# Masked attention with a residual: other slots for the indirect gathers, the copies that hold them and the searches ahead of them

## The chip, the cores and the metric

The kernel runs on one core of a Trainium2 chip. The metric is the device time in microseconds (us), lower is better. In the profiles PE is the matrix engine (PEld its weight loads), DVE the vector engine, ACT the scalar engine, POOL the general engine, and SP the engine whose queue issues most of the plain transfers. POOL issues the indirect transfers, in which a list of row numbers in SBUF says which rows of a DRAM tensor are read.

## The reference

`x` has 8 batches of 512 features by 1024 tokens, `cond_2048` is a mask of 8 by 1024 zeros and ones, and Wq and Wo are 512 by 512. There are 8 heads of 64 features.

```
xt = transpose(x, (0, 2, 1))
q = xt @ Wq.T                                   # queries, keys and values are the same
scores = einsum('bhqd,bhkd->bhqk', qh, qh) / sqrt(64)
logits = (scores * cmask + (1 - cmask) * -1e30) * rmask
attn = softmax(logits)
ctx = einsum('bhqk,bhkd->bhqd', attn, qh)
out = x + transpose(ctx @ Wo.T, (0, 2, 1))
```

A masked key has no weight in a kept row; a masked query has logits of zero everywhere, so that its context is the mean of all values. About half of the tokens are kept.

## The kernel before

Only kept tokens are attended. For every batch the kernel finds the kept tokens, gathers their rows of `x` and computes attention for up to 536 of them (a second version for 576 is in the program and isn't executed here). One further column stands for the mean token, which serves all masked queries. Rows of the result are added to `x` by another set of indirect transfers, which read for each of the 1024 tokens the row of its own kept place or the mean's row.

A **pair** is a batch and two of its eight heads: `(b, pr)` with pr 0 to 3, so there are 32. A pair has five **slots** c = 0 to 4. In slot c PE multiplies the scores of 128 keys (24 in the last) with all queries (`scores`, L684, the last one L698), ACT makes exponentials of them (`e`, `el`, L707), and PE weighs the values of the slots before (`weigh`, L731). Between these a pair's slots also prepare the next pair: in slots 0 and 1 its queries are projected (`pq`, L550) and copied to `qT` by ACT and DVE (L567); behind slot 2 PE turns `qT` into values (`turn_values`, L588) and DVE copies them to `v` (L597, two copies); then come their squares on ACT, the largest length on DVE (`len`, `top`), a small matmul (L628) and the bias `m`, `bias` (L637 to L641), which the next pair's first exponential needs.

Between the pairs' own work the function `plan` puts tasks into slots: `put(batch, pair, slot, task, ..., rank)`. Inside one slot tasks run in the order of their rank, with ranks under 5 ahead of the rest. The order of each engine's instructions is what `late` writes while it walks through pairs and slots; nothing is reordered later. An engine that waits holds everything behind it in its own row. The tasks that matter here are these:

- `search(n, i)` (DVE, L464 and L467): for piece i of batch n, i = 0 to 4, one pass over the token ranks counts and finds the source rows. The pass is over 1024, 896, 768, 640 and 512 columns for i = 0 to 4.
- `gather(n, i)` (POOL, L478): an indirect transfer `xin<-xd` of the rows that `search(n, i)` found. It stands for n = 2 to 7 in batch n-1. `collect(n, i)` turns the gathered piece on PE (L491) in the fourth slots of pairs 1 and 2 of the same batch.
- `wait_for_values(pair)` (POOL, L471): POOL copies two elements of row 0 of the pair's values `v` to a scratch tile `tick`. The copy can't run until DVE has written both halves of `v`, so POOL's later instructions are held until then.
- `fetch(b, i)` (POOL, L1084): an indirect transfer that adds rows of the output `od` of batch b to `g`, which `load_rows` has filled with rows of `x` two slots or more before. There are 8 per batch, for b = 0 to 4 in batch b+2. Later `finish_blocks(b, i)` (DVE, L1054) transposes `g` into `whole`, from which the result is stored.
- In every pair POOL also issues four small transfers `row<-rt` (L822), which carry the inverse sums of the pair before through DRAM. They wait for DVE's `rt` (L819).
- `half_product` (PE, L930, sixteen or eight matmuls of 256 columns) stands in the fourth slots; its sums are made by DVE (`joined`, L954) and written to `od` by POOL (L971).

Of the kernel before, what the change touches and what calls it, by code (L numbers as in the profile page):

```python
# [305 lines left out]
def attention_of_kept_tokens(ctx, tc, x, mask, wq, wo, out, ident, wqT, woT, verdict, flag):  # L306
# [7 lines left out]
    ND = D // P  # L314
# [6 lines left out]
    NC = -(-LONG // P)  # L321
    LAST = NC - 1
# [43 lines left out]
    xs, xbars, xmeans, xins, xcs, searches = {}, {}, {}, {}, {}, {}  # L366
# [106 lines left out]
    def gather(b, i):  # L473
        n = sizes[i]
        if i == 0:
            xins[b] = []
        xin = sb.tile([P, D], F32, tag="xin", name=f"xin_{b}_{i}", bufs=NC)
        nc.gpsimd.indirect_dma_start(  # L478
            out=xin[:n, :],
            out_offset=None,  # L480
            in_=rows_of_x[b],
            in_offset=bass.IndirectOffsetOnAxis(ap=searches[b][2][:n, i : i + 1], axis=0),
        )
        xins[b].append(xin)

    def collect(b, i, tag="t", copy=None):
        n = sizes[i]
# [842 lines left out]
    def plan():  # L1330
# [5 lines left out]
        def put(b, pr, c, task, *args, rank=0):  # L1336
            todo[b, pr, c].append((rank, task, args))
# [17 lines left out]
        for n in range(1, B):  # L1355
            if n == 1:
                turns = [(0, 0, 0), (0, 0, 1), (0, 0, 3), (0, 0, 4)]
                finds = [(0, 1, 0), (0, 1, 3), (0, 1, 3), (0, 1, 4), (0, 2, 0)]
                feats = [None] * (ND + 2) + [(0, 0, 4), (0, 1, 0)]
                takes = finds  # L1360
                means, mean = (0, 2, 1), (0, 2, 3)
                turned = [(0, 2, 3)] * NC
            else:
                b = n - 2
                if n == 2:
                    loads = [(0, 1, i) for i in range(NC)] + [(0, 2, i) for i in range(3)]
                    turns = [(0, 2, 3), (0, 2, 4), (0, 3, 1), (0, 3, 3)]
                    feats = [(0, 2, 3)] * 2 + [(0, 2, 4)] * 2
                    feats += [(0, 3, 0), (0, 3, 1), (0, 3, 2), (0, 3, 4)]
                else:  # L1370
                    loads = [(b, 0, i) for i in range(4)]
                    loads += [(b, 1, 0), (b, 1, 2), (b, 1, 4), (b, 2, 0)]
                    turns = [(b, 1, 1), (b, 2, 1), (b, 2, 3), (b, 3, 1)]
                    feats = [(b, 1, 1), (b, 1, 4), (b, 2, 1), (b, 2, 4), (b, 2, 4)]
                    feats += [(b, 3, 1), (b, 3, 4), (b, 3, 4)]
                for i in range(NN * A):
                    put(*loads[i], load_piece, n, i // A, i % A)
                put(b, 2, 0, load_ranks, n)
                finds = [(b + 1, 0, min(i, 3)) for i in range(NC)]
                takes = [(b + 1, 0, 0)] + [(b + 1, 0, 3)] * (NC - 1)  # L1380
                put(b + 1, 0, 3, wait_for_values, (b + 1, 1), rank=1)
                means, mean = (b + 1, 0, 1), (b + 1, 0, 3)
                turned = [(b + 1, 1, 3)] * 2 + [(b + 1, 2, 3)] * 2 + [(b + 1, 1, 3)]
            for i in range(NQ):
                put(*turns[i], turn, n, i, rank=6.8 if turns[i][2] == LAST - 1 else 1)
            for i in range(NN * ND):
                if feats[i]:
                    put(*feats[i], add_features, n, i, rank=1)
            for i in range(NC):
                put(*finds[i], search, n, i)  # L1390
                put(*takes[i], gather, n, i, rank=2)
                if i in (0, 2):
                    put(*turned[i], collect, n, i, rank=7)
                else:
                    put(*turned[i], collect, n, i, "t", nc.scalar.copy, rank=7.2)
            put(*means, mean_of, n)
            put(*mean, put_mean, n, rank=6.5)

        for b in range(B - 1):
            nxt = b + 1  # L1400
            steps = ((1, 2), (6, 5), (7, 4, LAST + P), (3,))
            at = [(nxt, 1), (nxt, 2), (nxt, 3), (nxt + 1, 0)]
            if b == B - 3:
                steps = ((1, 2), (6, 5, LAST + P), (7, 3, 4))
            elif b == B - 2:
                steps = ((1, 2, 6, 5, 4, 7, 3, LAST + P),)
            for i, step in enumerate(steps):
                for k in step:
                    task, k = (output, k - P) if k > P else (half_product, k)
                    put(*at[i], 3, task, b, k, rank=7.1)  # L1410
                    if b == B - 2 and task is half_product and k == 5:
                        for j in (2, 3):
                            put(*at[i], 3, mix_contexts, b, j, rank=7.1)
            if b < B - 2:
                put(nxt, 1, 3, mix_contexts, b, 0, rank=6.8)
                put(nxt, 1, 3, mix_contexts, b, 1, rank=6.8)
                put(nxt, 3, 2, mix_contexts, b, 2, rank=5.5)
                put(nxt, 3, 2, mix_contexts, b, 3, rank=5.5)
            else:
                for k in range(2):  # L1420
                    put(nxt, 1, 1 + k, mix_contexts, b, k, rank=5.5)
            if b < B - 3:
                after = [(nxt + 1, i // NC, i % NC) for i in range(4 * NC)]
                firsts, slots = after[3:], after[6:]
                ends = [(2, 0), (2, 3), (2, 3), (2, 4), (3, 0), (3, 3), (3, 3), (3, 3)]
                ends = [(nxt + 1, *at) for at in ends]
            elif b == B - 3:
                firsts = [(nxt, 2 + i // NC, i % NC) for i in range(2, 2 + NT)]
                slots = [(nxt + 1, 0, i // 2) for i in range(NT)]
                ends = [(1, 0), (1, 0)] + [(1, 3)] * (NT - 2)  # L1430
                ends = [(nxt + 1, *at) for at in ends]
            else:
                firsts = [(nxt, 1 + i // NC, i % NC) for i in range(NT)]
                slots = [(2, 1), (2, 1), (2, 2), (2, 3), (2, 4), (3, 0), (3, 0), (3, 1)]
                slots = [(nxt, *at) for at in slots]
                ends = [(nxt, 3, c) for c in (0, 0, 3, 3, 3, 3, 3, 3)]
            for i in range(NT):
                put(*firsts[i], load_rows, b, i, rank=1)
                put(*slots[i], fetch, b, i, rank=3)
            for i, at in enumerate(ends):  # L1440
                put(*at, finish_blocks, b, i, rank=(2, 2, 2, 6.8, 4.5)[at[2]])
# [16 lines left out]
    def late(n):  # L1458
# [7 lines left out]
        for i in range(NC):  # L1466
            gather(0, i)
# [25 lines left out]
        blank_share(pairs[0])  # L1493

        todo = plan()
        settled = defaultdict(list)
        for p in range(len(pairs) - 2):
# [154 lines left out]
```

## Time and profile before

| what | value |
|---|---|
| median of three runs | 663.98 us (663.39 to 664.54) |
| profiled execution | 657.5 us |
| its span | 655.7 us |
| mean granted clock of PE | 0.975 |
| PE busy | 595.9 us (91%) |
| DVE busy | 404.6 us (62%) |
| ACT busy | 349.0 us (53%) |
| POOL busy | 241.9 us (37%) |

The span is the time between the first and last instruction of the profiled execution. "Idle before, releaser" in a row of groups says how long the engine was idle just before these instructions and what ended most of that time. In a row of the timeline the first two numbers are start and duration in us, and the bracket holds the idle time just before. A row of windows gives a stretch, its length and each engine's busy time with its count of instructions, then PE's granted clock, the busy share of the transfer engines and GB/s. The stretches that are used run from the first exponential of a pair to that of the next.

### The profile page before, as it was taken

How to read it: one execution, taken by the hardware profiler on the slowest of the kernel's cores; microseconds unless marked ns; L12 is line 12 of the kernel's file. 1: busy time of each engine (PE TensorE's matmuls, PEld its weight loads, DVE VectorE, ACT ScalarE, POOL GpSimd, SP SyncE). 2: the span in 40 equal slices, each digit the busy share in tenths (PEclk: the TensorE clock that was granted, in tenths of full speed). 3: DMA queues.
4: the chain of work that ended last, by engine and by line, in shares of the span. 5: the costliest groups of instructions: out<-in, count | busy, mean ns of one | idle time of the engine just before them, and what ended most of it. 6: DMA issues, size and time to landing. Idle time of an engine off the chain costs nothing.

```text
span 655.7 us, 22452 instructions
## 1 busy us (share of the span) xinstructions
PE 595.9 (91%) x9296; PEld 446.3 (68%) x9296; DVE 404.6 (62%) x1191; ACT 349.0 (53%) x986; POOL 241.9 (37%) x327
## 2 busy tenths in 40 slices
PE   6689898999999999999989998999989999998862
PEld 4556765778777776788757785678757776785431
DVE  6546678556766677577755776467745564765242
ACT  5266686566555565556656564556545446436300
POOL 4501433211344334541453324551353525537040
PEclk9799999999999999999999998999999999999985
DMA  8746545422389758975887678774756648798555
GB/s 278 241 130 185 188 112 173 132 95 73 101 238 230 161 161 253 245 194 113 239 255 217 120 211 270 181 184 103 183 192 134 139 129 213 150 289 135 148 167 168
DMA packets 100161, 116.89 MB, mean 178 GB/s; under 512 B 13224, under 2 KB 67048, under 8 KB 100040
## 3 DMA queue, kind: packets, MB, share of 16 engines
q1 hardware_dynamic: 76176, 76.56, 39.6%
q0 software_dynamic: 19520, 36.58, 23.8%
q10 hardware_dynamic: 4344, 2.12, 1.1%
q8 instruction: 77, 1.26, 0.8%
q14 instruction: 44, 0.36, 0.2%
HBM read 72.68 MB, written 42.54 MB: 176 GB/s over the span
## 4 chain that ended last, share of the span: by engine, by line
PE 74%; DVE 7%; DMA 5%; issue 4%; POOL 3%; ACT 3%; SPq 1%; another core or an unknown queue 1%; DVEq 0%; POOLq 0%; ACTq 0%
PE av L731 17%; PE s L684 16%; PE pq L550 15%; PE ph L930 12%; DMA g<-od,origin 3%; PE v L588 3%; PE xc L491 3%; POOL g L1084 3%; PE s L698 2%; PE pa L987 2%; DVE junk L464 1%; DVE joined L954 1%; ACT e L707 1%; DMA out_dram<-whole 1%; DMA x<-in_x_dram 1%
## 5 line engine op out<-in xcount | busy, mean ns | idle before, releaser
L707 ACT ACTIVATE e<-s,bias 128x536 f32<-128x536 f32 x256 | 178.2, 700 | 64.0 <-PE s L684 55.9
L731 PE MATMUL av<-e,v 64*64 64x268 f32 x2048 | 168.3, 392 | 18.5 <-ACT el L707 4.8
L684 PE MATMUL s<-qT 64*64 64x268 f32 x2048 | 171.1, 390 | 4.1 <-ACT el L707 2.2
L822 POOL DMA_DIRECT2D row<-rt x120 | 63.1, 549 | 233.3 <-DVE rt L819 229.5
L550 PE MATMUL pq<-xc,wqT 64*64 64x268 f32 (+1 forms) x1984 | 136.0, 386 | 0.6 <-DVE m L637 0.4
L731 PEld LDWEIGHTS av<-e,v 64*64 64x64 f32 x2048 | 88.1, 133 | 55.6 <-ACT el L707 7.2
L684 PEld LDWEIGHTS s<-qT 64*64 64x64 f32 x2048 | 100.4, 133 | 30.1 <-ACT el L707 6.2
L550 PEld LDWEIGHTS pq<-xc,wqT 64*64 64x64 f32 x1984 | 97.3, 133 | 21.8 <-DVE m L637 2.2
L1084 POOL DMA_INDIRECT g<-od,origin x48 | 76.3, 1589 | 18.1 <-issue 14.3
L597 DVE COPY v<-v 128x320 f32<-128x320 f32 x64 | 28.4, 485 | 54.9 <-PE v L588 38.9
L707 ACT ACTIVATION_READ_ACCUMULATOR e<-s,bias 128x1 f32 x256 | 50.1, 196 | 0.0
L478 POOL DMA_INDIRECT xin<-xd,source x40 | 38.6, 965 | 26.8 <-issue 7.3
L707 ACT ACTIVATE el<-s,bias 128x268 f32<-128x268 f32 x64 | 30.3, 479 | 31.8 <-PE s L698 13.0
L464 DVE TENSOR_SCALAR_CACHE_REDUCE junk<-rank,key 128x1024 f32<-128x1024 f32 (+4 forms) x40 | 39.8, 996 | 2.8 <-DMA rank<-ranks 2.8
L954 DVE TENSOR_TENSOR joined<-ph,side 128x512 f32<-128x512 f32 x28 | 19.2, 690 | 35.0 <-PE ph L930 23.7
L427 ACT ACTIVATE junka<-x 128x512 f32<-128x512 f32 x64 | 40.2, 628 | 0.7
L930 PE MATMUL ph<-wo,mix 128*128 128x256 f32 x168 | 39.8, 385 | 0.2 <-DVE joined L954 0.2
L1054 DVE STREAM_TRANSPOSE whole<-g 128x512 f32<-128x512 f32 x56 | 36.4, 683 | 2.3 <-DMA g<-od,origin 2.2
L765 ACT COPY cT<-av 128x268 f32<-128x268 f32 x62 | 22.3, 383 | 28.4 <-PE av L731 28.3
L930 PEld LDWEIGHTS ph<-wo,mix 128*128 128x128 f32 x168 | 30.5, 190 | 7.5 <-issue 1.6
L971 POOL DMA_DIRECT2D od<-joined x14 | 10.9, 776 | 64.3 <-DVE joined L954 64.3
L401 DVE STREAM_TRANSPOSE xt<-x 128x1024 f32<-128x1024 f32 x28 | 34.2, 1224 | 0.2
(179 smaller groups left out, 813.4 us busy)
## 6 DMA issues: line engine op xcount, KB each, us to landing
xd<-xt SPq DMA_DIRECT2D x120, 128.0 KB
x<-in_x_dram SPq DMA_DIRECT2D x56, 256.0 KB
g<-xd SPq DMA_DIRECT2D x48, 256.0 KB
out_dram<-whole SPq DMA_DIRECT2D x20, 512.0 KB
rb<-row SPq DMA_DIRECT2D x60, 160.0 KB
od<-joined POOLq DMA_DIRECT2D x14, 512.0 KB
out_dram<-whole SPq DMA_DIRECT2D x16, 256.0 KB
rank<-ranks SPq DMA_DIRECT2D x7, 512.0 KB
```

Source lines behind the costliest of these rows:

```text
L401: nc.vector.transpose(xt.rearrange("p k (d f) -> p k d f", d=ND), xs[b][r][:, :, at : at + n].rearrange("p d (k t) -> p k d t", t=Q),)
L427: nc.scalar.activation(junk, xs[b][r][:, d, :], AF.Copy, accum_out=xbars[b][:, d, r : r + 1])
L464: nc.vector.tensor_scalar(junk[:, :n], rank[:, i * P :], key[:, col], 0.0, ALU.is_le, ALU.add, accum_out=found[:, col])
L478: nc.gpsimd.indirect_dma_start(out=xin[:n, :], out_offset=None, in_=rows_of_x[b], in_offset=bass.IndirectOffsetOnAxis(ap=searches[b][2][:n ...
L550: mm = nc.tensor.matmul(pqs[pair][hf][heads[h], :n], wqT[rows, d, at : at + DK], xcs[b][rows, d, hf * KH : hf * KH + n], start=(not cross ...
L684: nc.tensor.matmul(s[h][to, hf, :KH], qT[heads[h], at : at + DK], qT[heads[h], hf * KH : (hf + 1) * KH], start=True, stop=True,)
L707: act = nc.scalar.activation(e[:, h], of[h], AF.Exp, bias=biases[pair][:, c : c + 1], scale=SCALE, accum_out=acc[:, h, c : c + 1],)
L731: mm = nc.tensor.matmul(avs[pair][hf][heads[h], :KH], v[rows, c, heads[h]], e[rows, h, hf, :] if c < LAST else e[rows, h, :], start=(c == ...
L822: nc.gpsimd.dma_start(row[:, :, a, :].rearrange("h c j -> (h c) j"), rt[a * Q : a * Q + 2 * NC, :])
L930: nc.tensor.matmul(po[:, t * m : (t + 1) * m], left[:, i, t * P : (t + 1) * P], right[:, i, :], start=(i == 0), stop=(i == 1),)
L1054: nc.vector.transpose(whole.rearrange("p (d a) n -> p a d n", a=A)[:, :, :, i * Q : (i + 1) * Q], gs.pop((b, i)).rearrange("p (a d f) -> p ...
L1084: nc.gpsimd.indirect_dma_start(out=gs[b, i], out_offset=None, in_=ods[b], in_offset=bass.IndirectOffsetOnAxis(ap=origin[:, b, i : i + 1] i ...
```

## The change

Five things are changed in `plan` and one in `gather`.

- The five searches of batch n (n of 2 and more) stood in slots 0, 1, 2, 3, 3 of pair 0 of batch n-1. Now searches 0 and 1 stay, search 4 stands in slot 2, search 2 in slot 3, and search 3 in slot 4 at rank 4.6, behind the bias and share of the next pair.
- The five gathers stood in slot 0 (the first) and slot 3 (the other four) of pair 0. Now gather 0 stands in slot 0, gather 1 in slot 1, gathers 2 and 4 in slot 3, and gather 3 in slot 0 of pair 1.
- `wait_for_values` stood in slot 3 of pair 0 alone. Now it stands in slot 3 of pairs 0, 1 and 2.
- The eight fetches of b = 0 to 4 stood one to a slot in slots 1 to 4 of pair 1 and 0 to 3 of pair 2. Now three stand in slot 3 of pair 1, one in slot 0 of pair 2, three in slot 3 of pair 2 and one in slot 0 of pair 3. Their transposes and loads stay.
- `xins[b]` becomes a dictionary, since gathers no longer come in the order of i.

```diff
     def gather(b, i):
         n = sizes[i]
         if i == 0:
-            xins[b] = []
+            xins[b] = {}
...
-        xins[b].append(xin)
+        xins[b][i] = xin
...
-                finds = [(b + 1, 0, min(i, 3)) for i in range(NC)]
-                takes = [(b + 1, 0, 0)] + [(b + 1, 0, 3)] * (NC - 1)
-                put(b + 1, 0, 3, wait_for_values, (b + 1, 1), rank=1)
+                finds = [(b + 1, 0, c) for c in (0, 1, 3, 4, 2)]
+                takes = [(b + 1, 0, 0), (b + 1, 0, 1), (b + 1, 0, 3), (b + 1, 1, 0), (b + 1, 0, 3)]
+                for pr in range(ND - 1):
+                    put(b + 1, pr, 3, wait_for_values, (b + 1, pr + 1), rank=1)
...
             for i in range(NC):
-                put(*finds[i], search, n, i)
+                put(*finds[i], search, n, i, rank=4.6 if n > 1 and finds[i][2] == LAST else 0)
                 put(*takes[i], gather, n, i, rank=2)
...
             if b < B - 3:
                 after = [(nxt + 1, i // NC, i % NC) for i in range(4 * NC)]
-                firsts, slots = after[3:], after[6:]
+                firsts = after[3:]
+                slots = [(1, 3)] * 3 + [(2, 0)] + [(2, 3)] * 3 + [(3, 0)]
+                slots = [(nxt + 1, *at) for at in slots]
```

PE's, ACT's and SP's rows keep their order. The first place is POOL's row in pair 0 of a batch, from the `row` transfers of the pair before to the output's `joined`; `xin_0` to `xin_4` are the five gathers of the next batch, `tick_1` the copied element of pair 1's values. Before:

```order
L822 DMA row_3_3702<-rt_3_3700 10x32 x4
L478 DMA xin_0_3712<-xd_97,source_3171 128x512
L471 COPY tick_1_3848<-v_1_3789 1x2
L478 DMA xin_1_3852<-xd_97,source_3171 128x512
L478 DMA xin_2_3854<-xd_97,source_3171 128x512
L478 DMA xin_3_3856<-xd_97,source_3171 128x512
L478 DMA xin_4_3858<-xd_97,source_3171 24x512
L971 DMA od_3581<-joined_0_3049 128x2x512
```

Now the same stretch reads:

```order
L822 DMA row_3_3710<-rt_3_3708 10x32 x4
L478 DMA xin_0_3720<-xd_97,source_3176 128x512
L478 DMA xin_1_3750<-xd_97,source_3176 128x512
L471 COPY tick_1_3855<-v_1_3799 1x2
L478 DMA xin_2_3859<-xd_97,source_3176 128x512
L478 DMA xin_4_3861<-xd_97,source_3176 24x512
L971 DMA od_3589<-joined_0_3055 128x2x512
```

One gather has moved ahead of the copied element, two are left behind it, and `xin_3` is gone from the stretch. The second place is POOL's row in pairs 1 to 3 of the same batch, where `g_0` to `g_7` are the eight fetches and `row_0` to `row_2` the row transfers. Before:

```order
L822 DMA row_0_3968<-rt_0_3966 10x32 x4
L1084 DMA g_0_3850<-od_3581,origin 128x512
L1084 DMA g_1_3894<-od_3581,origin 128x512
L1084 DMA g_2_3975<-od_3581,origin 128x512
L1084 DMA g_3_4001<-od_3581,origin 128x512
L822 DMA row_1_4241<-rt_1_4239 10x32 x4
L1084 DMA g_4_4051<-od_3581,origin 128x512
L1084 DMA g_5_4105<-od_3581,origin 128x512
L1084 DMA g_6_4167<-od_3581,origin 128x512
L1084 DMA g_7_4251<-od_3581,origin 128x512
L822 DMA row_2_4510<-rt_2_4508 10x32 x4
L971 DMA od_4656<-joined_1_4647 128x2x512
```

Now:

```order
L822 DMA row_0_3974<-rt_0_3972 10x32 x4
L478 DMA xin_3_3983<-xd_97,source_3176 128x512
L471 COPY tick_2_4111<-v_2_4060 1x2
L1084 DMA g_0_3857<-od_3589,origin 128x512
L1084 DMA g_1_3897<-od_3589,origin 128x512
L1084 DMA g_2_3981<-od_3589,origin 128x512
L822 DMA row_1_4250<-rt_1_4248 10x32 x4
L1084 DMA g_3_4009<-od_3589,origin 128x512
L471 COPY tick_3_4385<-v_3_4334 1x2
L1084 DMA g_4_4058<-od_3589,origin 128x512
L1084 DMA g_5_4113<-od_3589,origin 128x512
L1084 DMA g_6_4177<-od_3589,origin 128x512
```

Each of pairs 1 and 2 now has one transfer directly behind its `row` transfers and three behind a copied element. The third place is what follows on POOL, and there the eighth fetch has moved into pair 3, behind the third set of row transfers:

```order
L822 DMA row_2_4521<-rt_2_4519 10x32 x4
L1084 DMA g_7_4260<-od_3589,origin 128x512
L971 DMA od_4668<-joined_1_4659 128x2x512
L886 DMA od_4668<-oc_4_4670 24x128 x4
L822 DMA row_3_4789<-rt_3_4787 10x32 x4
```

On DVE only the searches move, by up to a slot and a half within pair 0, as the first of the points above says.

## The prediction

> **What bounds the kernel.** I read the page's chain first, then its groups, to see who waits for PE where PE is the chain:
>
> ```profile
> PE 74%; DVE 7%; DMA 5%; issue 4%; POOL 3%; ACT 3%; SPq 1%; another core or an unknown queue 1%; DVEq 0%; POOLq 0%; ACTq 0%
> ...
> L1084 POOL DMA_INDIRECT g<-od,origin x48 | 76.3, 1589 | 18.1 <-issue 14.3
> L597 DVE COPY v<-v 128x320 f32<-128x320 f32 x64 | 28.4, 485 | 54.9 <-PE v L588 38.9
> ```
>
> PE carries three quarters of the chain, and DVE's value copies stand idle 38.9 us for its value matmuls. What the change moves, POOL's gathers (1589 ns each in L1084's row), is hardly on the chain, so they mostly act through what PE, DVE and ACT do while POOL makes descriptors. The timeline shows such an action. Here is pair 2 of batch 2 and then the same place in batch 3:
>
> ```profile
> 215.32 0.23 PE L588 MATMUL v<-ident,qT 64*64 64x64 f32 x2
> 213.47 1.66 POOL L1084 DMA_INDIRECT g<-od,block_origin  x1 [0.30 <-DMA g<-xd]
> 215.43 1.58 POOL L1084 DMA_INDIRECT g<-od,block_origin  x1 [0.30 <-DMA xd<-xt]
> 216.86 0.89 DVE L597 COPY v<-v 128x320 f32<-128x320 f32 x2 [3.15 <-PE s L684]
> 287.72 0.23 PE L588 MATMUL v<-ident,qT 64*64 64x64 f32 x2
> 288.06 0.89 DVE L597 COPY v<-v 128x320 f32<-128x320 f32 x2 [1.95 <-PE v L588]
> 288.33 1.65 POOL L1084 DMA_INDIRECT g<-od,origin  x1 [2.77 <-DMA xd<-xt]
> ```
>
> In batch 2 the last value matmul ends at 215.55, and an idle DVE starts its copy only at 216.86, 1.31 us later and at the end of the gather that began at 215.43. In batch 3 POOL was held up until 288.33 by chance; the copy came 0.11 us behind the matmul (287.95 to 288.06). So PE's completion reaches others late while a gather is being issued. The stretches of the pairs (pair 2 of batches 2, 3, 5 and 6, then pair 3 of batch 2, which has no gather) give the price:
>
> ```profile
> 207.07:226.24 19.17, 18.48 (x293) 14.34 (x289) 12.50 (x33) 11.38 (x33) 8.46 (x8) 1.00 0.92 222
> 279.47:297.43 17.96, 17.96 (x292) 14.60 (x288) 12.49 (x33) 11.25 (x33) 8.45 (x8) 1.00 0.76 191
> 427.65:446.82 19.17, 18.46 (x294) 13.99 (x289) 12.50 (x33) 11.37 (x34) 8.45 (x8) 1.00 0.75 179
> 502.08:522.03 19.95, 19.03 (x318) 14.80 (x314) 10.43 (x31) 9.71 (x29) 10.60 (x12) 1.00 0.53 114
> 226.24:244.00 17.76, 17.76 (x312) 14.33 (x308) 13.62 (x36) 10.88 (x34) 4.93 (x9) 1.00 0.42 117
> ```
>
> Batches 3 and 5 do the same work with the same transfer share (0.76, 0.75). Where all four fetches came behind the copy, the pair took 17.96 us and PE never stood idle; where the first two preceded it, 19.17. That is 1.2 us for the place alone. Fetches in the fourth slot cost nothing there.
>
> **What each pair loses now.** Pair 0, batches 1 to 6:
>
> ```profile
> 101.47:118.31 16.84, 13.99 (x276) 9.46 (x272) 12.19 (x43) 8.75 (x26) 7.06 (x10) 1.00 0.57 173
> 172.10:188.94 16.84, 16.06 (x282) 11.66 (x277) 12.77 (x44) 8.84 (x27) 7.83 (x11) 1.00 0.49 135
> 244.00:261.02 17.02, 16.19 (x281) 11.79 (x276) 12.77 (x44) 8.83 (x26) 7.86 (x11) 1.00 0.82 251
> 315.20:332.86 17.66, 15.68 (x272) 11.11 (x267) 13.19 (x48) 8.94 (x27) 7.84 (x11) 1.00 0.84 264
> 388.94:408.50 19.56, 16.34 (x276) 11.87 (x272) 12.85 (x45) 8.95 (x26) 7.84 (x11) 0.91 0.87 273
> 464.57:483.02 18.45, 16.04 (x270) 11.19 (x266) 13.19 (x47) 8.94 (x26) 7.84 (x11) 1.00 0.75 240
> ```
>
> Their floor I build from pair 3, whose 17.76 us hold two half-products and a small output; pair 0 has one half-product (none in batch 1). The chain prices these:
>
> ```profile
> 236.25 3.65 PE ph L930 x16
> 239.90 1.01 PE po L874 x32
> 254.36 1.92 PE ph L930 x8
> ```
>
> 17.76 - 3.65 - 1.01 + 1.92 = 15.0; with an allowance of 0.3 (estimate) for the mean's products the floor is 15.3, and 13.4 in batch 1. Pair 0 is above it by 3.4, 1.5, 1.7, 2.4, 4.3 and 3.1 us, 16.4 in all. Where it goes is seen in batch 2; the last rows are batch 6, where the first gather came late:
>
> ```profile
> 178.40 1.02 POOL L478 DMA_INDIRECT xin<-xd,source  x1 [0.30 <-PE s L684]
> 181.34 0.17 POOL L471 COPY tick<-v 1x2 f32<-1x2 f32 x1 [1.92 <-DVE v L597]
> 182.04 0.98 POOL L478 DMA_INDIRECT xin<-xd,source  x1 [0.53 <-issue]
> 186.32 0.48 ACT L707 ACTIVATE el<-s,bias 128x268 f32<-128x268 f32 x1 [3.06 <-PE s L698]
> 472.01 1.04 POOL L478 DMA_INDIRECT xin<-xd,source  x1 [0.57 <-DMA out_dram<-whole]
> 474.68 0.18 POOL L471 COPY tick<-v 1x2 f32<-1x2 f32 x1 [1.63 <-DVE v L597]
> ```
>
> The four held gathers start at 182.04 and take about 1 us each with 0.3 between, so to about 186.9, over the single half-product and into the last slot, and ACT stands 3.06 us before `el`. Pair 1, batches 1 (no fetch), 2 and 6, and batch 2's first fetch there:
>
> ```profile
> 118.31:136.32 18.01, 17.59 (x282) 14.56 (x278) 10.89 (x31) 11.38 (x33) 2.12 (x4) 1.00 0.39 122
> 188.94:207.07 18.13, 17.56 (x282) 14.73 (x278) 10.38 (x30) 11.39 (x33) 8.40 (x8) 1.00 0.85 212
> 195.56 1.67 POOL L1084 DMA_INDIRECT g<-od,block_origin  x1 [0.30 <-issue]
> 483.02:502.08 19.06, 18.34 (x292) 13.91 (x288) 8.73 (x27) 10.28 (x28) 8.40 (x8) 1.00 0.62 147
> ```
>
> The six stretches of pair 1 sum to 3.8 us above 18.01 each. The five of pair 2 are 1.2, 0, 1.4, 1.2 above 17.96 and, in batch 6 with more products, 0.9 by its length less PE's time (19.95 - 19.03): 4.7. All told 16.4 + 3.8 + 4.7 = 24.9 us of removable loss.
>
> **The change, priced.**
>
> - *Gathers two and four of pair 0 stay in the fourth slot, four become two.* Half of the loss there would be 1.3 us a batch by the mean (16.4 / 6 / 2), 0.75 by the smallest. I take 1.0, nearer the lower, since it is the later gathers, reaching into the last slot, that go. Six batches: 6.0 stays.
> - *Four lone gathers a batch*: `xin_1` in pair 0 and `xin_3` in pair 1 (6 batches each), `g_3` in pair 2 and `g_7` in pair 3 (5 each), 22 in all. Each starts where POOL gets to it, behind the row transfers or the gather ahead: from 6.4 us into the pair (213.47 - 207.07) to 7.6 (`xin_1` behind `xin_0`: 178.40 + 1.02 + 0.30 - 172.10). That is near the value copies. Call the price k. Low end: pair 1 of batch 2, whose fetch began 6.6 us in, lost 0.12 (18.13 - 18.01). High end: 1.2, from pair 2, where a second gather followed. Less than zero is excluded, since a lone gather takes no work away from where it starts. Between them lies batch 6: the gather began 7.44 in, and the copied element came 10.11 in against 9.24 in batch 2, 0.87 later. I take the middle, k = 0.65: 14.3.
> - *Three fetches behind a copied element in pairs 1 and 2*: nothing, by the 17.96 stretch; their cover is the two half-products of that slot.
> - *Twelve more copied elements*, 0.17 us each on POOL: nothing. Queued behind a waiting one are the gathers of that slot, later the `od` transfers and the next `row` transfers, which come a full slot later.
> - *Searches*, moved within pair 0 on DVE, which is busy 12.8 of 16.8 us there: nothing of their own, the last two leave the place ahead of `joined`. Search 3 (about 0.9 us) now delays the next inverse sums and the row transfers by as much, within the bounds of k.
> - *The dictionary*: no instruction.
>
> Sum: before 24.9, after 6.0 + 14.3 = 20.3, so -4.6 us. The profiled execution would come from 657.5 to 652.9; the median of the runs is 6.5 us above it, which I carry over unchanged: 663.98 - 4.6 = 659.4.
>
> **Late fetches.** A fetch started later also lands later, and DVE's transposes wait for it:
>
> ```profile
> 230.83 2.14 POOL L822 DMA_DIRECT2D row<-rt  x4 [10.13 <-DVE rt L819]
> 236.39 1.89 DVE L1054 STREAM_TRANSPOSE whole<-g 128x512 f32<-128x512 f32 x3
> 239.93 0.69 DVE L954 TENSOR_TENSOR joined<-ph,side 128x512 f32<-128x512 f32 x1 [0.44 <-PE ph L930]
> 601.66 5.57 DMA g<-od,origin
> ```
>
> `g_7` would start at 230.83 + 2.14 + 0.3 = 233.3, and be wanted by the third transpose at 237.65, 4.4 us later. The chain's tail shows 5.57 us to a landing behind 1.5 us of issue, among other fetches; alone I expect it shorter, so some 1 to 2.7 us late. DVE's first idle time behind it is only 0.44, but the next pair's bias is not due until 244; I cost it at nothing up to about 1.5 us of lateness.
>
> **Rivals.**
>
> - *The lone gathers hit the values everywhere* (slower). Place: behind the row transfers in all four pairs, pair 3 included, which is clean now. The sum is 22k + 6.0 against 24.9: it turns at k = 0.86, and k = 1.2 gives 32.4, +7.5, so 671.5. For it: batch 6's 0.87. Against: one gather's 1.6 us is over by the values' end where it starts at 6.4.
> - *They hit nothing* (faster still): k = 0.12 leaves 8.6, -16.3, so 647.7. For it: batch 2's pair 1.
> - *`g_7` is late beyond the slack* (slower): 2.7 us late costs 1.2 a batch more, +6.0 over five, 665.4; a slower landing more. It decides from about 0.9 a batch, 2.4 us late. For it: the tail's 5.57. Against: pair 3's transfer share, 0.42, is the lowest of the stretches shown.
> - *Issue of gathers delays no other engine* (no change). The waits then belong to transfer load, which stays, and the time is 664.0. Against: 17.96 and 19.17 at the same share.
>
> The page "SBUF — State Buffer" of the Trainium skill, section "SBUF: two separate sides", is of this last rival's side: engine and DMA ports are disjoint and "PE, ACT, and DVE's dedicated pair never wait on anyone". By that rule moving the gathers would change nothing, 664.0; the 1.31 us between matmul and copy speaks against taking it as the whole account here, though it needn't be SBUF that delays the completion.
>
> **Chances.** A measurement of this kernel tells about 0.2% (1.3 us) from no change. My forecast, k of 0.4 to 0.8: 0.50. Gathers that hit nothing: 0.13. No change, by the fourth rival or by k between 0.8 and 0.9: 0.12. Lone gathers that hit everywhere: 0.15. `g_7` late: 0.10. So faster 0.63, same 0.12, slower 0.25. The forecast alone spans 654 (k = 0.4) to 662.7 (k = 0.8). The range leaves out the outer parts of both ends: 650.5 to 669.
>
> **What would show it.** Right: pairs 1 and 2 at 18.0 to 18.7, pair 3 up from 17.76 by k, pair 0 at 16.3 to 17; `tick` three times a batch with DVE's copy behind PE by under 0.7 us. Wrong: copies over 1 us behind their matmuls in all four pairs (k); DVE idle ahead of L1054 in pair 3 (`g_7`); pair lengths as before (fourth rival).

## The result, and the profile after

The changed kernel took 654.25 us (median of 4 runs, 653.23 to 657.58) and the kernel before 664.26 us (663.39 to 669.43, 4 runs). The ratio is 0.9893, with a 95% interval of 0.9845 to 0.994. On another chip it was 0.9884 (0.9831 to 0.9937). The profiled execution went from 657.5 to 653.2 us, its span from 655.7 to 651.5. So the profiles are 4.2 us apart, and the runs about 7 (by the ratio) to 10 (by the medians).

The page after, the same parts as before:

```profile
span 651.5 us, 22484 instructions
...
PE 70%; DVE 8%; DMA 7%; issue 7%; POOL 3%; ACT 3%; SPq 1%; DVEq 0%; POOLq 0%; ACTq 0%
...
L597 DVE COPY v<-v 128x320 f32<-128x320 f32 x64 | 28.4, 486 | 64.4 <-PE v L588 61.7
...
L588 PE MATMUL v<-ident,qT 64*64 64x64 f32 x1280 | 34.5, 222 | 9.0 <-issue 8.3
...
L1054 DVE STREAM_TRANSPOSE whole<-g 128x512 f32<-128x512 f32 x56 | 37.1, 687 | 4.5 <-DMA g<-od,origin 3.9
```

The value copies don't wait less than before, they wait more (64.4 us in all, from 54.9), and PE itself stands 8.3 us inside its value matmuls for nothing that the profile shows. Before, that was 1.5 us:

```profile
L588 PE MATMUL v<-ident,qT 64*64 64x64 f32 x1280 | 30.3, 221 | 2.1 <-issue 1.5 <-DVE qm L574 0.6
```

The windows of the changed kernel, pairs 0 to 3 of batch 2 and then pairs 0 and 3 of batch 5, tell where the gain is:

```profile
172.73:189.59 16.86, 15.65 (x276) 11.64 (x271) 11.88 (x41) 8.86 (x27) 6.91 (x10) 1.00 0.48 124
189.59:208.33 18.74, 17.91 (x288) 14.21 (x284) 11.29 (x33) 11.39 (x34) 8.48 (x9) 1.00 0.72 198
208.33:226.45 18.12, 18.12 (x293) 14.61 (x289) 12.50 (x33) 11.38 (x33) 8.65 (x9) 1.00 0.92 220
226.45:245.33 18.88, 17.97 (x312) 14.37 (x308) 13.70 (x36) 10.90 (x34) 6.63 (x10) 1.00 0.57 139
389.99:406.63 16.64, 15.60 (x276) 11.66 (x271) 11.88 (x41) 8.85 (x27) 6.89 (x10) 1.00 0.82 244
443.43:461.77 18.34, 18.00 (x312) 14.41 (x308) 13.65 (x36) 10.90 (x34) 6.62 (x10) 1.00 0.55 126
```

Pair 2 fell from 19.17 to 18.12 us in batch 2, pair 0 from 19.56 to 16.64 in batch 5, where no stretch at half clock is left; pair 3 rose from 17.76 to 18.88 and 18.34. Summed over batches 1 to 6, with the prediction's terms beside them:

| us against the kernel before | predicted | measured |
|---|---|---|
| pair 0 | -6.5 (-16.4 + 6.0 + 6k) | -5.3 |
| pair 1 | +0.1 (-3.8 + 6k) | +1.0 |
| pair 2 | -1.4 (-4.7 + 5k) | -4.7 |
| pair 3 | +3.2 (5k) | +4.1 |

Together these pairs are about 4.8 us shorter; the rest of the span is 0.6 us longer.

What a lone gather did is in the timeline of batch 2: `xin_1` in pair 0, `xin_3` in pair 1, `g_3` in pair 2, `g_7` in pair 3, each with the value matmuls or the value copy beside it.

```profile
180.36 0.98 POOL L478 DMA_INDIRECT xin<-xd,source  x1 [0.30 <-issue]
182.01 0.44 PE L588 MATMUL v<-ident,qT 64*64 64x64 f32 x12 [0.57 <-issue]
182.60 0.89 DVE L597 COPY v<-v 128x320 f32<-128x320 f32 x2 [1.86 <-PE v L588]
196.92 1.03 POOL L478 DMA_INDIRECT xin<-xd,source  x1 [0.30 <-issue]
198.13 0.34 PE L588 MATMUL v<-ident,qT 64*64 64x64 f32 x4 [0.43 <-issue]
198.56 0.89 DVE L597 COPY v<-v 128x320 f32<-128x320 f32 x2 [2.43 <-PE v L588]
214.73 1.65 POOL L1084 DMA_INDIRECT g<-od,block_origin  x1 [0.30 <-issue]
216.95 0.89 DVE L597 COPY v<-v 128x320 f32<-128x320 f32 x2 [1.98 <-PE v L588]
233.47 1.65 POOL L1084 DMA_INDIRECT g<-od,block_origin  x1 [0.30 <-issue]
235.20 0.89 DVE L597 COPY v<-v 128x320 f32<-128x320 f32 x2 [2.15 <-PE v L588]
239.13 0.71 DVE L1054 STREAM_TRANSPOSE whole<-g 128x512 f32<-128x512 f32 x1 [0.62 <-DMA g<-od,block_origin]
```

From their pairs' starts the copies come at 9.87, 8.97, 8.62 and 8.75 us; where no gather is near, they came at about 8.3 in pair 0, 7.95 in pair 1 (batch 1), 8.6 in pair 2 and 8.15 in pair 3. So `g_3`, over at 8.05 while the value matmuls end at 8.48, cost nothing, and the other three, which are issued when those matmuls should come to their end, cost 1.6, 1.0 and 0.6. The delay has another form here than in the kernel before. In 19 of the 22 pairs with a lone gather the copy comes within 0.14 us of the last value matmul, so it is PE that is late: it even stops between its value matmuls (0.57 and 0.43 us in the rows above). In the other three the copy lags by 0.20, 0.74 and, in pair 0 of batch 6, 2.66 us.

### The profile page after: what moved, and what is told of

Same layout as the page of the kernel before. It is cut to its first block, busy times and chain, and to the rows that moved or that the text cites. A ratio compares the mean times of both kernels' runs of the same rounds, so it can differ in the third digit from the quotient of the medians.

```text
span 651.5 us, 22484 instructions
## 1 busy us (share of the span) xinstructions
PE 594.8 (91%) x9296; PEld 447.9 (69%) x9296; DVE 404.9 (62%) x1191; ACT 348.7 (54%) x986; POOL 247.4 (38%) x339
## 4 chain that ended last, share of the span: by engine, by line
PE 70%; DVE 8%; DMA 7%; issue 7%; POOL 3%; ACT 3%; SPq 1%; DVEq 0%; POOLq 0%; ACTq 0%
PE av L731 16%; PE s L684 15%; PE pq L550 14%; PE ph L930 10%; DMA g<-od,origin 4%; PE v L588 3%; PE xc L491 2%; PE s L698 2%; PE pa L987 2%; POOL g L1084 2%; ACT e L707 1%; POOL row L822 1%; DMA od<-joined 1%; PE po L874 1%; DVE joined L954 1%
## 5 line engine op out<-in xcount | busy, mean ns | idle before, releaser
L731 PE MATMUL av<-e,v 64*64 64x268 f32 x2048 | 164.6, 390 | 10.2 <-ACT el L707 5.9
L684 PE MATMUL s<-qT 64*64 64x268 f32 x2048 | 165.1, 389 | 0.9 <-ACT e L707 0.4
L550 PE MATMUL pq<-xc,wqT 64*64 64x268 f32 (+1 forms) x1984 | 134.3, 386 | 0.3
L731 PEld LDWEIGHTS av<-e,v 64*64 64x64 f32 x2048 | 86.0, 132 | 47.6 <-ACT el L707 8.7
L684 PEld LDWEIGHTS s<-qT 64*64 64x64 f32 x2048 | 98.2, 133 | 22.8 <-ACT e L707 3.3
L550 PEld LDWEIGHTS pq<-xc,wqT 64*64 64x64 f32 x1984 | 97.1, 133 | 20.6 <-DVE m L637 1.7
L597 DVE COPY v<-v 128x320 f32<-128x320 f32 x64 | 28.4, 486 | 64.4 <-PE v L588 61.7
L588 PEld LDWEIGHTS v<-ident,qT 64*64 64x64 f32 x1280 | 31.5, 134 | 16.4 <-issue 13.2
L588 PE MATMUL v<-ident,qT 64*64 64x64 f32 x1280 | 34.5, 222 | 9.0 <-issue 8.3
L707 ACT ACTIVATE el<-s,bias 128x268 f32<-128x268 f32 x64 | 30.4, 480 | 19.0 <-PE s L698 15.5
```

The lines of the kernel that those rows point to most:

```text
L550: mm = nc.tensor.matmul(pqs[pair][hf][heads[h], :n], wqT[rows, d, at : at + DK], xcs[b][rows, d, hf * KH : hf * KH + n], start=(not cross ...
L588: nc.tensor.matmul(pts[h][to, c * DK : (c + 1) * DK], qT[heads[h], at : at + DK], ident[heads[h], heads[h]], start=True, stop=True,)
L684: nc.tensor.matmul(s[h][to, hf, :KH], qT[heads[h], at : at + DK], qT[heads[h], hf * KH : (hf + 1) * KH], start=True, stop=True,)
L707: act = nc.scalar.activation(e[:, h], of[h], AF.Exp, bias=biases[pair][:, c : c + 1], scale=SCALE, accum_out=acc[:, h, c : c + 1],)
L731: mm = nc.tensor.matmul(avs[pair][hf][heads[h], :KH], v[rows, c, heads[h]], e[rows, h, hf, :] if c < LAST else e[rows, h, :], start=(c == ...
```

## The experiments

The theory, sharpened by this, is one of place: a gather costs where PE's work ends, or should start, while POOL is issuing it, and otherwise nothing. The rivals are load (the transfers themselves delay), landing (the last fetch is late), and POOL work of any kind. The runs were made in four groups, each on a chip of its own; ratios are to the kernel before on the same chip.

### The two halves apart

The fetches and their copied elements alone, on the kernel before:

```diff
-                firsts, slots = after[3:], after[6:]
+                firsts = after[3:]
+                slots = [(1, 3)] * 3 + [(2, 0)] + [(2, 3)] * 3 + [(3, 0)]
+                slots = [(nxt + 1, *at) for at in slots]
...
-                put(b + 1, 0, 3, wait_for_values, (b + 1, 1), rank=1)
+                for pr in range(ND - 1):
+                    put(b + 1, pr, 3, wait_for_values, (b + 1, pr + 1), rank=1)
```

> The kernel before with the fetches in their new slots and the copied elements of all three pairs; gathers and searches as before. Lengths of pairs are summed over batches 1 to 6, against the kernel before. If a gather costs only where the value matmuls end while it is being issued (the theory of the place): pair 1 loses its 3.8 us of excess, pair 2 4.7, pair 3 gains 4.1 as in the changed kernel, pair 0 stays; span 651.3, 4.4 us under the kernel before. If the waits came from the transfers' load, which is the same: no pair moves by over 1 us, and the span is 655.7.

The gathers and searches alone are the changed kernel with these lines undone:

> The changed kernel with the fetches in their old slots and the copied element of pair 0 alone. Theory of the place: pair 0 takes the changed kernel's lengths (5.3 us less than before in all), pairs 2 and 3 stay as before, and pair 1, where gather 3 now precedes four unheld fetches, loses 1 to 4 us; span 652 to 655. If the parts don't add up, the sum of this run's and the fetches' run's differences is not the changed kernel's -4.2 within 2 us, once pair 1 is taken out.

Measured: 665.97 us against 667.08 (ratio 0.9964, 0.9919 to 1.0009) and 666.05 us (0.9994, 0.9951 to 1.0037). Neither half alone can be told from no change. Pairs 0, 2 and 3 do in the part that is meant for them what they do in the whole: with the fetches alone pair 2 is 4.8 us shorter and pair 3 3.6 longer, with the gathers alone pair 0 is 5.2 shorter. Against the load theory, pair 2 moves by 1.2 to 1.3 us in each of four batches with the same transfers.

As whole spans the parts don't add up. They are 9.1 and 4.9 us longer than the kernel before's profile, where both together are 4.2 shorter. Of these 14.0 us pair 1 takes 9.2, pair 0 of the fetches' run 3.6 and the last batch of that run 6.2. Two misses are behind it. With the gathers alone pair 1 grew by 8.5 us, not 1 to 4. Its window in batch 2, and from the timeline the unheld first fetch and the copy (`remote` marks a wait whose end the profile can't name):

```profile
189.38:209.80 20.42, 19.21 (x288) 14.51 (x284) 11.23 (x33) 11.40 (x33) 9.39 (x9) 1.00 0.81 216
```

```profile
198.36 1.61 POOL L1084 DMA_INDIRECT g<-od,block_origin  x1 [0.30 <-DMA xd<-xt]
200.11 0.89 DVE L597 COPY v<-v 128x320 f32<-128x320 f32 x2 [3.93 <-remote]
```

The fetch behind `xin_3` covers the values a second time, and the copy comes 10.7 us in. The halves need each other here: the copied element in pair 1 takes this away.

The other miss: the fetches alone left pair 0 with its four held gathers, and it came out at 17.0 to 20.6 us, 3.6 us above the kernel before's profile in all. Pair 1, which was to lose 3.8 us, took 0.7 more. From the timeline of pair 0 in batch 3 the last of the four gathers, PE's matmuls, and DVE's waiting copy and sum, and then a window of 3.41 us behind them:

```profile
260.23 0.90 POOL L478 DMA_INDIRECT xin<-xd,source  x1 [0.30 <-issue]
258.04 1.99 PE L930 MATMUL ph<-woT,mix 128*128 128x256 f32 x8
262.45 0.17 DVE L507 TENSOR_SCALAR xc<-mean 128x4 f32<-128x4 f32 x1 [5.09 <-remote]
262.55 0.69 DVE L954 TENSOR_TENSOR joined<-ph,side 128x512 f32<-128x512 f32 x1
259.97 0.68 PE L698 MATMUL s<-qT 64*64 64x268 f32 x8
263.29 1.57 PE L731 MATMUL av<-e,v 64*64 64x268 f32 x16 [2.64 <-DVE joined L954]
```

```profile
263.90:267.31 3.41, 3.41 (x44) 2.11 (x40) 1.97 (x12) 0.58 (x2) 0.43 (x1) 0.51 1.04 364
```

Four gathers run over the half-product, the last until 261.13. `joined` starts 2.52 us behind the half-product's last matmul (260.03 to 262.55), PE is idle for 2.64 us, and the granted clock is half for 3.41 us from 0.6 us after PE's return on. So lateness behind a row of gathers is larger than behind one. In the profile of the kernel before `joined` lags by 3.09 us in batch 5, right ahead of its stretch at half clock, and by 0.63 to 0.82 in batches 2, 3, 4 and 6. In the changed kernel, whose two held gathers end just ahead of the half-product, it lags by 0.04 us in all five. Apart from the start and the end of each execution, this run had four stretches at half clock (three behind pair 0), the profile of the kernel before one, that of the changed kernel none.

### The lone gathers that cost, held

The last fetch behind the three of pair 2's slot 3:

```diff
-                slots = [(1, 3)] * 3 + [(2, 0)] + [(2, 3)] * 3 + [(3, 0)]
+                slots = [(1, 3)] * 3 + [(2, 0)] + [(2, 3)] * 4
```

> The changed kernel with the last fetch in slot 3 of pair 2 behind the other three, so that no gather is left in pair 3. Theory of the place: pair 3 goes back to 17.75 us in batches 2 to 5 (it is 18.3 to 18.9), pair 2 stays at 18.0 although four fetches now reach to its end; 4.1 us less, span 647.4. If pair 3 lost its time to something else than this gather: no change, 651.5. If the fourth fetch costs in pair 2 or in pair 3's first slot what it saves: 651 or more.

And gather 3 as well, behind the fetches of pair 1's slot 3:

```diff
-                takes = [(b + 1, 0, 0), (b + 1, 0, 1), (b + 1, 0, 3), (b + 1, 1, 0), (b + 1, 0, 3)]
+                takes = [(b + 1, 0, 0), (b + 1, 0, 1), (b + 1, 0, 3), (b + 1, 1, 3), (b + 1, 0, 3)]
...
-                put(*takes[i], gather, n, i, rank=2)
+                put(*takes[i], gather, n, i, rank=2 if i != 3 else 3.5)
```

> The changed kernel with the last fetch held as in the run before, and gather 3 held too, behind the three fetches of pair 1's slot 3. Theory of the place: pair 1 from 18.7 to 18.9 back to 18.0 in all six batches (4.6 us), pair 3 to 17.75 (4.1 us), others as they are; span about 642.8. If a fourth gather in the slot costs as much there as in pair 0: only the pair 3 part, about 647. Load theory: 651.5.

Measured on the chip of the two halves: 653.27 us, ratio 0.9797 (0.9702 to 0.9892), and 649.51 us, 0.9724 (0.9632 to 0.9816). Pair 3 with the last fetch held, then pairs 1 and 3 with both held, batch 2:

```profile
226.40:244.10 17.70, 17.70 (x306) 14.58 (x308) 14.04 (x39) 10.70 (x33) 4.55 (x9) 1.00 0.60 140
```

```profile
188.99:207.47 18.48, 18.07 (x290) 14.24 (x286) 11.30 (x33) 11.39 (x33) 8.47 (x9) 1.00 0.77 193
225.80:243.50 17.70, 17.70 (x309) 14.51 (x305) 13.71 (x36) 10.85 (x33) 4.92 (x9) 1.00 0.60 144
```

Pair 3 is back at its floor (4.2 us in all, as expected), and the four fetches cost pair 2 only 1.0. Pair 1 fell to 18.5, not to 18.0: 2.2 us of the 4.6. Its slot 2 is back at 2.39 us, but its slot 0 takes 3.56 where it took 3.20 in batch 1, and the next group shows 18.37 as this pair's length where none of its gathers delays it. The floor of 18.0 that the prediction took was too low. The spans (651.1 and 649.0) missed the expected 647.4 and 642.8 by more than the pairs did: the last batch was 2.6 and 3.5 us longer than in the changed kernel's profile. The changed kernel itself wasn't run on this chip. Against its ratios elsewhere (0.9893 and 0.9884) only the interval of the run with two held lies clear of theirs.

### Searches, a third held gather, other POOL work, a later transpose

The searches in their old slots:

```diff
-                finds = [(b + 1, 0, c) for c in (0, 1, 3, 4, 2)]
+                finds = [(b + 1, 0, min(i, 3)) for i in range(NC)]
```

> The changed kernel with the searches in their old slots, so that search 3 no longer stands ahead of the next inverse sums on DVE. Theory of the place: the row transfers of pair 0 leave about 0.9 us earlier, gather 3 starts near 6.5 us into pair 1 in place of 7.4 and is over by 7.6, ahead of the values' end near 7.9; pair 1 falls from 18.7 to 18.9 to about 18.1 (some 4 us in all), pair 0 loses up to 0.3 a batch by two searches ahead of joined; span 648 to 650. If the price went by the gather's being there and not by its place: no change in pair 1, 651.5.

Gather 1 held too (on the kernel with two held):

```diff
-                takes = [(b + 1, 0, 0), (b + 1, 0, 1), (b + 1, 0, 3), (b + 1, 1, 3), (b + 1, 0, 3)]
+                takes = [(b + 1, 0, 0), (b + 1, 0, 3), (b + 1, 0, 3), (b + 1, 1, 3), (b + 1, 0, 3)]
```

> The run with two held, and gather 1 held as well, as the first of three behind pair 0's copied element. Theory of the place: the value copy of pair 0 comes at 8.3 us in place of 9.6 to 9.9, which gives 1.4 us a batch, and a third gather over the half-product and the last slot takes some of it back (four cost 2.6 a batch in the kernel before, two 0.5 now), so pair 0 moves by -1 to +1 us a batch; the span is 640 to 652 by that. Stretches at half clock at the end of pair 0, which the kernel before and the run with the fetches alone show and the others don't, come back if three gathers there are enough for them.

Other POOL work in the places of the two that were held:

```diff
+    def plain_rows(b):
+        t = sb.tile([P, 2, Q], F32, tag="plain", name=f"plain_{b}", bufs=1)
+        for k in range(2):
+            nc.gpsimd.dma_start(t[:, k, :], rows_of_x[b][:P, k * Q : (k + 1) * Q])
+
+    def copies(b):
+        t = sb.tile([P, Q], F32, tag="fill", name=f"fill_{b}", bufs=1)
+        for k in range(8):
+            nc.gpsimd.tensor_copy(t, quadrant.unsqueeze(2).to_broadcast([P, A, Q // A]))
...
+                put(b + 1, 1, 0, plain_rows, n, rank=2)
+                put(b + 1, 3, 0, copies, n, rank=3)
```

> The run with two held, with other POOL work in the two places that the gathers left: in pair 1, at about 7 us, two plain transfers of 128 short rows each (batches 1 to 6), and in pair 3, at about 7 us, eight small copies of POOL that take about 1.5 us (batches 1 to 6). If only the issue of an indirect transfer holds back what PE completes: pair lengths as in the run with two held (pair 1 18.0 to 18.5, pair 3 17.7), 649. If any transfer of POOL does: pair 1 up by 0.7. If any work of POOL does: pair 3 up by 0.6 as well, together 8 us.

The last transpose one slot later (on the changed kernel):

```diff
-                ends = [(2, 0), (2, 3), (2, 3), (2, 4), (3, 0), (3, 3), (3, 3), (3, 3)]
+                ends = [(2, 0), (2, 3), (2, 3), (2, 4), (3, 0), (3, 3), (3, 3), (3, 4)]
```

> The changed kernel with the transpose of the last fetch one slot later, in slot 4 of pair 3. It tells apart what the last fetch costs pair 3 by its place and by its late landing. By the profile 0.3 to 0.5 us of pair 3's loss lie in slot 3 in batches 2 to 4 (DVE waits for the landing) and 0.6 in slot 2 (the value copy). If so: slot 3 back to 6.4 us, slot 2 stays at 3.1, 1.2 us less in all, span 650.3. If the whole loss is the value copy's: no change; if all is the landing's: 4 us less.

These four fell on another chip, and there little came out as expected: the kernel before itself took 639.89 us (31 runs, 636.7 to 644.75). Against it: searches back 644.4 us (1.0069, 1.0033 to 1.0106), a third held 638.21 (0.997, 0.9934 to 1.0007), other POOL work 639.55 (1.0003, 0.9971 to 1.0035), transpose later 643.8 (1.0064, 1.0041 to 1.0087). The trace of the last one, pair 3 of batch 2, shows why:

```profile
228.26 0.23 PE L588 MATMUL v<-ident,qT 64*64 64x64 f32 x2
227.44 1.65 POOL L1084 DMA_INDIRECT g<-od,block_origin  x1 [0.30 <-issue]
228.62 0.89 DVE L597 COPY v<-v 128x320 f32<-128x320 f32 x2 [1.60 <-PE v L588]
```

The gather covers the end of the value matmuls (228.49) exactly as in the changed kernel, takes the same 1.65 us, and the copy comes 0.13 us later. On this chip PE's completions aren't late beside `g_7`. They aren't wholly on time: with `xin_1` still lone, the copies of pair 0 lag by 0.24 to 0.39 us in this run, and PE stops 0.40 to 0.73 us inside its value matmuls in batches 3 to 6. Where the lone gathers are held, the pairs are at their floors; pairs 0 and 3 of batch 2 with the third held gather, then pair 3 with the searches back, and in the timeline of the same run the transpose of `g_7`:

```profile
170.00:185.29 15.29, 15.12 (x276) 11.49 (x272) 11.93 (x41) 8.84 (x27) 6.89 (x10) 1.00 0.43 117
221.66:239.42 17.76, 17.76 (x312) 14.43 (x308) 13.60 (x36) 10.89 (x34) 4.92 (x9) 1.00 0.60 147
```

```profile
222.02:240.62 18.60, 17.83 (x310) 14.43 (x306) 13.71 (x36) 10.89 (x34) 6.62 (x10) 1.00 0.57 137
```

```profile
234.37 0.71 DVE L1054 STREAM_TRANSPOSE whole<-g 128x512 f32<-128x512 f32 x1 [0.87 <-DMA g<-od,block_origin]
```

15.29 is the prediction's floor of pair 0. With `g_7` lone in pair 3 its late landing alone cost 3.7 us over five batches there: slot 3 took 6.7 to 7.5 us in place of 6.4 (7.1 in batch 6), and the copy was on time. The later transpose removed that (pair 3 at 17.75). Against the run with the searches back it lost 1.0 us in pair 0 (15.5 to 16.3 us), whose first gather started 0.6 us later in batches 3 to 5, and 3.9 us in the last batch, the cause of which is open. Whether the searches' move pays where completions are late wasn't settled: gather 3 did start at 6.34 in place of 7.33, as expected, but there was nothing to gain.

### Is it the chip? The two kernels again, and POOL work again

No edit to the three kernels:

> The changed kernel once more, on another chip. On the chip of the last four runs the completions of PE were not late beside a gather, and pair 0 stood at its floor. If that is a property of the chip, there are two cases. On a chip with late completions: the pair lengths of the first result, and 1 to 2% under the kernel before. On one without: pair 0 at 15.3 to 16.3 in both kernels, pair 3 0.3 to 1.1 us a batch above 17.75 by the late landing of the last fetch, nothing gained in pair 2, and the changed kernel 0 to 1% over the kernel before (about 643 against 640). If the last four runs were quick for their edits alone: the first result's lengths, whatever the chip.

> The kernel before once more, for its trace on the same chip. With late completions: pair 2 at 19.2, pair 0 at 16.8 to 20.6 with stretches at half clock behind it, 660 to 668. Without: value copies within 0.15 us of their matmuls wherever a gather is being issued, pair 0 about 15.4, pair 2 18.0, pair 1 18.0 to 18.4, and 638 to 641.

> The run with other POOL work in the places that the gathers left, once more on this chip. With late completions: if only an indirect transfer's issue holds them back, pair 1 18.4 to 18.5 and pair 3 17.7 as in the run with two held; if any transfer's does, pair 1 up by 0.4 to 0.7; if any POOL work does, pair 3 up by 0.6. Without late completions nothing can be told: pair 1 18.37, pair 3 17.75 again.

Measured, on a third chip: the changed kernel 655.85 us against 663.23 (0.9884), with the pair lengths of the first result within 0.6 us in batches 1 to 6; the kernel before, profiled, 669.73 us; with the two gathers held and other POOL work in their places 646.41. So completions are late here. In the kernel before, batch 3, the timeline of PE, then the last of these rows as it was in the first profile, and then the windows of pair 0 and of the half-clock stretch:

```profile
262.51 0.68 PE L698 MATMUL s<-qT 64*64 64x268 f32 x8
267.13 2.06 PE L731 MATMUL av<-e,v 64*64 64x268 f32 x16 [3.94 <-DVE joined L954]
```

```profile
257.71 1.13 PE L731 MATMUL av<-e,v 64*64 64x268 f32 x16 [0.81 <-DVE joined L954]
```

```profile
250.47:271.29 20.82, 16.88 (x272) 12.13 (x268) 13.35 (x48) 8.96 (x26) 7.86 (x11) 0.87 0.87 280
265.70:272.53 6.83, 5.39 (x56) 3.20 (x60) 4.15 (x14) 2.49 (x8) 0.80 (x1) 0.50 0.83 310
```

Pair 0 took 20.82 us here and 17.02 in the first profile. PE is idle for 3.94 us where it was 0.81 there, and 6.83 us at half clock begin within that idle time; this execution had four such stretches, three of them behind pair 0. The changed kernel had one on this chip, 6.83 us in its last batch, so they aren't the kernel before's alone. The other POOL work, in pair 1 and pair 3 of batch 2:

```profile
195.30 1.11 POOL L489 DMA_DIRECT2D plain<-xd  x2
195.73 0.75 PE L598 MATMUL v<-ident,qT 64*64 64x64 f32 x40
196.57 0.89 DVE L607 COPY v<-v 128x320 f32<-128x320 f32 x2 [1.73 <-PE v L598]
231.77 2.12 POOL L494 COPY fill<-quadrant 128x32 f32<-128x32 f32 x8
232.13 0.80 PE L598 MATMUL v<-ident,qT 64*64 64x64 f32 x40
233.07 0.89 DVE L607 COPY v<-v 128x320 f32<-128x320 f32 x2 [1.41 <-POOL fill L494]
```

The copies of POOL cover the values' end (232.93) and the value copy comes 0.14 us behind it: these copies hold nothing back. Of the plain transfers the issue ends 0.07 us ahead of the last value matmul, so they test PE's issue (40 matmuls in one run, no stop) more than its last completion. Pairs 1 and 3 were at 18.5 and 17.7 in batches 2 to 5, as with two held. So of the work that POOL did here, it is the issue of indirect transfers that delays. This rests on one execution, and for plain transfers on the weaker test; by which path the issue reaches PE no run shows.

The third held gather once more:

> The run with gather 1 held as well, once more, on whatever chip. With late completions: pair 0's value copy at 8.3 us in place of 9.6 to 9.9, slot 2 back from 4.1 to 4.3 us to 2.6 to 2.8, and three held gathers in slots 3 and 4. If a third costs there what the kernel before shows for four (slot 3 at 5.3 to 6.9 us against 3.7 with two), pair 0 is at 17 to 18 in place of 16.7 and half-clock stretches come back: 650 to 655. If the first two explain the loss there, pair 0 is at 15.5 to 16.2: 640 to 645. Without late completions: 638, 0.3% under the kernel before.

It fell on a fourth chip, one without late completions: 640.49 us against 640.46 (1.0004, 0.9975 to 1.0033), pair 0 at 15.3 to 15.8 in batches 2 to 6. In batch 2 `joined` comes 0.04 us behind the half-product although a gather is being issued there. What three gathers over the half-product cost where completions are late stays open.

## Why the prediction was right, point by point

- **What bounds, and how gathers act.** Right that a gather's issue delays what PE hands on; 1.2 to 1.3 us for the place alone came back in four batches of the fetches' run. Incomplete in the form: in the changed kernel most of the loss is PE stopping and ending late, with the copy on time behind it, and behind four held gathers `joined` lagged by up to 3.1 us, which the sum had only as a mean excess. That the effect depends on where the kernel runs couldn't be seen in one profile.
- **The sum.** -4.6 us predicted for the profiled execution, -4.2 measured; that they agree so well is luck, since two terms were too high and two too low. *Two of four gathers left in pair 0's fourth slot* was mis-sized: 1.0 us a batch expected, about nothing measured in batch 2, where slots 3 and 4 took 3.69 and 2.48 us, and 3.75 and 2.48 on the chip without lateness. Too high as well was `g_3` (3.2 us expected in all, none measured); too low were `xin_1` and `g_7`, below. A small slip beside it: 16.4 / 6 / 2 is 1.4, not 1.3, which the term that was taken doesn't use.
- **One k for all lone gathers** failed as a form. Measured by place: `xin_1` 1.4 to 1.7 us, `xin_3` up to 1.0 at the copy (of which pair 1 kept about 0.4 above its real floor), `g_3` 0, `g_7` 0.6 and its landing 0.3 to 0.5 more. The rows shown had the rule already: a gather over by 8.06 doesn't cover the end of matmuls that end at 8.48.
- **Pair 1's floor** of 18.0 was taken from a batch without gathers; on the chips without lateness it is 18.4, by a slot 0 of 3.56 us in place of 3.20. Why slot 0 differs wasn't found.
- **`g_7`'s landing** was costed at nothing. It cost 0.3 to 0.5 us a batch in three of five batches, and more on the chip where the copies were on time. In batch 2 DVE waits 0.62 us for the landing, and slot 3 grows by 0.48. The rival was right in its mechanism, its slack of 1.5 us too generous.
- **The searches, dictionary and copied elements** at nothing: nothing in the traces speaks against it for the last two. The searches' move delays `xin_3`, which starts 7.33 us into pair 1 and 6.34 with the searches back; 7.33 is on the value matmuls. What that costs where completions are late wasn't measured.
- **The median carried over unchanged** is the step that failed in size: 4.6 us expected, 7 to 10 measured. The kernel before was profiled in an execution of 657.5 us, below the whole of its runs (663.39 to 664.54 then, 662.24 to 672.84 on the next chip), while the changed kernel's profile lies 1.0 us under its median. On the next chip the runs of the kernel before have a mean granted clock of 0.960 to 0.976, the low end in the longest (672.84 us) and the high end in the shortest; two profiles show that behind pair 0 with its four held gathers come stretches at half clock. The first profile had one such, at 404 us; the removal of others, which don't come in every execution, wasn't in the sum. The later profile of the kernel before, an execution of 669.73 us, was longer than the first by 2.4 us in pair 0 and 3.7 in pair 1 (batches 1 to 6), 2.8 in batch 0 and 2.5 in the last. That such losses are what made 654.25 of 659.4 (inside the range) is likely, but not shown: of the first three runs, at 663 to 665 us, there is no profile.
- **The fourth rival (issue delays nobody)** and with it the rule of the Trainium skill's page "SBUF — State Buffer", section "SBUF: two separate sides": the chips of two groups nearly agree with it (on one 0.13 us from matmul to copy beside `g_7` and up to 0.5 beside `xin_1`, on the other 0.04 from half-product to `joined`), the first profile (1.31) and the chips of the two other groups don't. The rule can't be the whole account of either.

On a chip without late completions the changed kernel itself wasn't run. Its two variants with a lone `g_7` were 0.6 to 0.7% slower than the kernel before there, those with it held the same within 0.4%. So the gain looks like one of chips that delay, and the version with two held gathers like the better one on both: 0.9724 where completions are late, and with other POOL work added 1.0003 where they aren't. None of the four groups shares its chip with another, so that the chip makes the difference, and not the occasion, isn't shown.

## What to carry to other kernels

Place an indirect transfer of POOL by what PE finishes while it is being issued, not by which slot has room: read when the matmuls end that another engine waits for, and keep the gather's one to two microseconds off that moment; hold it there with a copy that depends on the consumer's result. Don't hold so many that they cover the next handover: four behind one copy delayed `joined` by up to 3.8 us, two by 0.04. Look also at the other end, the first reader of what is fetched. And before carrying a profile's difference over to a median, see where the profiled execution lies among the runs: an execution below all of them may lack stalls that the others have.

## What was unexpected of the hardware

- The same kernel before took 640 us on two chips and 663 to 667 in the other three sets of runs. On one of the former a value copy beside `g_7` came 0.13 us behind its matmul. On the latter copies in the kernel before came up to 1.5 us late, `joined` behind four gathers up to 3.8, and in the changed kernel PE stopped among its value matmuls (8.3 us in L588's group). The gather's own duration is the same, 1.65 us. What differs between the chips wasn't found.
- An idle PE of 2.64 us was enough for a stretch at half clock, and so was one of 1.83 us (the changed kernel's second profile, 544.65 to 546.49, half clock from 547.42 on). An idle PE of 2.41 us (the first profile of the kernel before, 112.58 to 115.00) wasn't followed by one. These stretches lasted 3.41 or 6.83 us. The Trainium skill, page "TensorE: Matmul & The Clock Gate", Part 1, has a free-running window of 3413 ns, which agrees with these lengths, and puts the drop behind at least one idle window of about 3.4 us; the 2.64 and 1.83 us here are shorter than that.
